# Two convolution layers on Trainium2: an order pinned around each pair of tiles, and first-image sums of squares on ScalarE

## The chip, the cores and the metric

The kernel runs on one core of one Trainium2 chip. The metric is the device time of one execution in microseconds (us). A core has these engines, each with its own instruction queue that is worked through in order: TensorE (PE in the profile; its weight loads are listed as PEld), VectorE (DVE), ScalarE (ACT), GpSimd (POOL), and SyncE (SP), which here only issues DMAs. Matmul results go to PSUM; everything else lives in SBUF. Engines wait for one another through semaphores.

## The reference

The network adds four "pre-activation" layers to x, which has shape (4, 8, 512, 512): four images of eight channels.

```
x = x + L0(gn(x))       # spiking attention block
x = x + L1(gn(x))       # 13x13 depthwise convolution
x = x + L2(gn(x))       # 3x3 convolution on values rounded to integers
x = x + L3(gn(x))       # 3x3 convolution in float32

def gn(v, G=4, eps=1e-5):          # group norm: per image, over 2 channels x 512 x 512
    m, s = mean(v), var(v)
    return (v - m) / sqrt(s + eps)

def L2(x):
    sx, sw = 127 / max|x|, 127 / max|weight|
    return conv3x3(clip(round(x * sx)), clip(round(weight * sw))) / (sx * sw) + bias
```

The change lies in layers 2 and 3, and touches nothing before them. Layer 3 of an image needs the mean and the variance of the whole image after layer 2, for each group of channels.

## The kernel before

**Tiles.** Layers 2 and 3 cut each image into 85 windows of 8 rows by 8 channels (64 partitions); two windows make a tile of 128 partitions by 512 columns, and two tiles (a and b) make a pair. An image has 22 pairs, the last of which has one half-filled tile. In this text pair 2.7 is pair 7 of image 2, counted from 0, and n = 22 t + p numbers the pairs over all images: 88 in all.

**One pair through layer 2.** `load` (L951) brings the pair in, six pairs deep. `normalise` makes two copies on GpSimd that undo a column permutation (u, L965; four buffers) and one normalisation over both tiles on ScalarE (y, L969; two buffers). `quantise` rounds y to integers in bf16 on VectorE (xq, L980; three buffers). `layer2` multiplies each tile with a banded weight matrix in 6 matmuls (L997) into PSUM (three banks), and VectorE then scales each result and adds it to u (L1003, `scalar_tensor_tensor`), which leaves the pair's result in x3, a ring of 26 pairs. Statistics of that result: for tile a, `bn_stats` on VectorE (L1014); for tile b, a row sum that L1003 writes out on the side, and a row sum of squares from an `activation` with `Square` on ScalarE (L1009).

**Layer 3.** When an image is through, `norm3` (L1047 to L1078, with the helper at L175 to L195) turns the statistics into a mean, a scale, and scaled weights (band_t). `layer3` of a pair sets two edge columns (L1089, GpSimd), runs 12 float32 matmuls (the profile shows each as two, so 24 lines of L1096), and ScalarE adds a constant (o, L1105; ten buffers); SyncE stores the result (L1112). Rows that neighbouring windows share are exchanged inside x3 by DMAs that GpSimd issues (L1143).

**The loop.** One Python loop over n (L1122) traces, in this order: the load of pair n+5, `normalise` of n+2, `quantise` of n+1, `layer2` of n, and, from n = 25 on, `layer3` of pair n-25. So layer 3 of image t runs beside layer 2 of image t+1, and layer 3 of image 3 is left for the end. The build does not keep the order of the trace: it places each engine's instructions by its own estimate, within data dependences and within edges that the source asks for. `tc.issue_after(op)` asks for such an edge: what is traced in its block stands behind `op` on the engine of `op`. It is an order in the queue alone, no wait. Before, `layer2` of n stands behind `normalise` of n+2 on ScalarE and behind `quantise` of n+1 on VectorE; nothing keeps these two from being placed earlier still.

**What reuse of buffers ties together.** L1003 of pair n writes the ring place that layer 3 of pair n-26 has read, so it waits for those matmuls. The first tile of pair n+2 takes the PSUM bank that L1003 left with tile b of pair n.

Of the kernel before, what the change touches and what calls it, by code (L numbers as in the profile page):

```python
# [42 lines left out]
P = 128  # L43
# [768 lines left out]
def weights23(tc, i, pool, scratch, ps_1, ident):  # L812


    nc = tc.nc

    def col(name, n=1):
        return pool.tile([P, n], F32, name=name)

    n_taps = 3 * B  # L820
    w = {}
    c24 = pool.tile([n_taps, i["c24"].shape[1]], F32, name="c24")
    nc.scalar.dma_start(c24, i["c24"])
    w2 = pool.tile([n_taps, n_taps], F32, name="w2t")
    nc.scalar.dma_start(w2, i["w2"])
    w3 = pool.tile([n_taps, n_taps], F32, name="w3t")
    nc.scalar.dma_start(w3, i["w3"])
    w["b2"], b3 = col("b2"), col("b3")
    nc.scalar.dma_start(w["b2"], i["b2"])
    nc.scalar.dma_start(b3, i["b3"])  # L830
    w["b23"] = col("b23")
    nc.vector.tensor_add(w["b23"], w["b2"], b3)

    def banded(taps, dtype, name, firsts):

# [15 lines left out]
        return band  # L851

    w["band3"] = band3 = banded(w3, F32, "band3", (-1, 1))
    w["sum3"] = pool.tile([P, 2, HALF], F32, name="sum3")
    nc.vector.tensor_add(w["sum3"], band3[:, :, 0, :], band3[:, :, 1, :])
    nc.vector.tensor_add(w["sum3"], w["sum3"], band3[:, :, 2, :])
    w["eye3"] = pool.tile([P, 2, 3, HALF], F32, name="eye3")
    nc.vector.memset(w["eye3"], 0.0)  # L860
    nc.vector.tensor_add(
        w["eye3"][:, 0, 1, B:], ident[:, : HALF - B], ident[:, HALF : P - B]
    )
    nc.vector.tensor_add(
        w["eye3"][:, 1, 1, : HALF - B], ident[:, B:HALF], ident[:, HALF + B :]
    )

    wall = scratch.tile([P, 2, D], F32, tag="y", name="wall")
    wall = wall.rearrange("p n d -> p (n d)")[:, : n_taps * n_taps]
    nc.scalar.dma_start(wall, bass.AP(i["w2"].tensor, 0, [[0, P], [1, n_taps * n_taps]]))  # L870
    w["sw"] = sw = col("sw")
    nc.vector.tensor_reduce(sw, wall, AX.X, ALU.max, apply_absolute_value=True)
    nc.vector.reciprocal(sw, sw)
    nc.vector.tensor_scalar_mul(sw, sw, MAX_Q)
    nc.vector.tensor_scalar_mul(w2, w2, sw[:n_taps])
    nc.vector.tensor_scalar(w2, w2, MAX_Q, -MAX_Q, op0=ALU.min, op1=ALU.max)
    nc.vector.tensor_scalar(w2, w2, ROUND, ROUND, op0=ALU.add, op1=ALU.subtract)
    w["band2"] = banded(w2, BF16, "band2", (0,))


    w["xq"] = [pool.tile([P, 2, D + 4], BF16, name=f"xq_{j}") for j in range(3)]
    for xq in w["xq"]:
        nc.gpsimd.memset(xq, 0.0)
    w["st3"] = [pool.tile([P, W2_N, 6], F32, name=f"st3_{j}") for j in range(2)]
    for st3 in w["st3"]:
        nc.gpsimd.memset(st3, 0.0)

    w["sums"] = [pool.tile([P, 2, N_PAIRS], F32, name=f"sums_{j}") for j in range(2)]
    w["inv"] = col("inv")
    w["m"], w["r"] = col("m_own", T), col("r_own", T)  # L890
    w["mr"] = col("mr_own", T)
    return w


def layers23(
# [80 lines left out]
    def quantise(t, p):  # L976
# [6 lines left out]
        ready[t, p] = u, xq  # L983
        return op.ins

    def layer2(t, p):
        ks = tiles(p)
        n_p = HALF * len(windows(ks[-1]))
        u, xq = ready.pop((t, p))
        s0 = slot(t, p)  # L990
        st3 = w["st3"][t % 2]
        for j, k in enumerate(ks):
            ps = ps_2.tile([P, D], F32, tag="conv2", name="ps_conv2")
            for dx in range(3):
                for a, _ in windows(k):
                    half = slice(a * HALF, (a + 1) * HALF)
                    mm = nc.tensor.matmul(  # L997
                        ps[half, :], lhsT=w["band2"][half, 0, dx, :], rhs=xq[half, j, dx + 1 : dx + 1 + D],
                        start=dx == 0, stop=dx == 2,
                    )  # L1000
            own = x3[:n_p, s0 + j, 1 : D + 1]
            sums = w["sums"][t % 2][:, :, p : p + 1]
            nc.vector.scalar_tensor_tensor(  # L1003
                own, ps[:n_p, :], w["inv"][:n_p], u[:n_p, j, :], op0=ALU.mult, op1=ALU.add,
                accum_out=sums[:, 0, :] if j else None,
            )
            if j:
                square = wpool.tile([P, D], BF16, tag="square", name="square")
                nc.scalar.activation(  # L1009
                    square, own, AF.Square, bias=w["m"][:, t : t + 1], scale=-1.0,  # L1010
                    accum_out=sums[:, 1, :],
                )
            else:
                nc.vector.bn_stats(st3[:n_p, k, :], own)  # L1014
        return mm.ins

    pairs = x3[:, :, 1 : D + 1].rearrange("p (n j) d -> p n j d", j=2)
# [24 lines left out]
    def norm3(t):  # L1042


        st3 = w["st3"][t % 2]
        total, squares = (w["sums"][t % 2][:, j, : N_PAIRS - 1] for j in range(2))
        nc.vector.tensor_scalar_mul(total, total, 1.0 / D)  # L1047
        for h in range(2):
            nc.vector.tensor_copy(st3[:, 1::2, 3 * h + 1], total)
        nc.vector.tensor_scalar(total, total, w["m"][:, t : t + 1], None, op0=ALU.subtract)  # L1050
        nc.vector.tensor_mul(total, total, total)
        nc.vector.scalar_tensor_tensor(
            total, total, -1.0 * D, squares, op0=ALU.mult, op1=ALU.add
        )
        for h in range(2):
            nc.vector.tensor_scalar_mul(st3[:, 1::2, 3 * h + 2], total, 0.5)
        st3 = st3.rearrange("p k (h z) -> p (k h) z", z=3)
        nc.vector.tensor_scalar_add(st3[:, :, 1], st3[:, :, 1], w["b2"])  # L1058
        m, r = yield from group_steps(
            st3.unsqueeze(1), 1, W2_N * 2, mask2, avg_same, ps_1, f"x3_{t}"  # L1060
        )
        zero = wpool.tile([P, 1], F32, tag="zero", name="zero")
        nc.vector.tensor_sub(zero, m, w["b2"])
        band = wpool.tile([P, 2, 3, HALF], F32, tag="band", name="band_t")
        nc.vector.scalar_tensor_tensor(
            band, w["band3"], r, w["eye3"], op0=ALU.mult, op1=ALU.add
        )
        scaled = wpool.tile([P, 1], F32, tag="scaled", name="scaled")
        nc.vector.tensor_mul(scaled, zero, r)
        yield  # L1070
        ps = ps_1.tile([P, 1], F32, tag="misc", name="ps_const")
        for a in range(2):
            half = slice(a * HALF, (a + 1) * HALF)
            nc.tensor.matmul(
                ps[half, :], lhsT=w["sum3"][half, a, :], rhs=scaled[half, :], start=True, stop=True
            )
        const = wpool.tile([P, 1], F32, tag="const", name="const")
        nc.vector.tensor_sub(const, w["b23"], ps)  # L1078
        norms[t] = zero, band, const
        yield  # L1080
# [37 lines left out]
    n_chunk = N_PAIRS // 2  # L1118
    copies, at_once = [], 0
    n_all = T * N_PAIRS  # L1120
    norms, norm = {}, iter(())
    for n in range(n_all + N_PAIRS + LAG):  # L1122
        if n < n_all:
            for m in range(6) if n == 0 else [n + 5]:
                if m < n_all:
                    load(*divmod(m, N_PAIRS))


            for m in range(3) if n == 0 else [n + 2]:
                if m < n_all:  # L1130
                    first = normalise(*divmod(m, N_PAIRS))
            for m in range(2) if n == 0 else [n + 1]:
                if m < n_all:
                    then = quantise(*divmod(m, N_PAIRS))
            with tc.issue_after(first), tc.issue_after(then):
                did = layer2(*divmod(n, N_PAIRS))
        next(norm, None)
# [49 lines left out]
```

## Time and profile before

| what | value |
| --- | --- |
| time, median of 3 runs (lowest to highest) | 3051.62 us (3049.63 to 3054.68) |
| the profiled execution's own time | 3049.44 us |
| its span, first to last instruction | 3047.7 us |
| layer 0: 0 to 2131 us of the span | PE busy 2093.4 of 2131.0 us |
| layer 1: 2131 to 2582 us | PE busy 449.0 of 451.0 us |
| layer 2 of image 0, and its statistics: 2582 to 2683 us | PE busy 50.1, DVE 92.0, ACT 51.8, POOL 70.7 of 101.0 us |
| layer 2 of images 1 to 3 beside layer 3 of images 0 to 2: 2683 to 2983 us | PE busy 261.8, DVE 208.4, ACT 192.2, POOL 195.2 of 300.0 us |
| layer 3 of image 3: 2983 to 3047.7 us | PE busy 59.7 of 64.7 us |

The span is the time between the first and the last instruction that the profiler recorded; the execution's own time is 1.7 us longer. "Busy" is the time in which an engine works on at least one instruction. The table says where to look: in layers 0 and 1 TensorE has next to no idle time, and the change leaves them alone. In the first image of layer 2 VectorE is the busy engine. In the 300 us that follow TensorE is busiest and yet idle for 38 us.

### The profile page before, as it was taken

What the parts mean: (1) busy time and instruction counts of PE and PEld (TensorE: products, weight loads), DVE (VectorE), ACT (ScalarE), POOL (GpSimd) and SP (SyncE); (2) the same over time, 40 slices, a digit from 0 to 9 for tenths busy, and PEclk for the clock granted to TensorE, in tenths of its full rate; (3) what the DMA queues carried; (4) which work ended last, traced back from release to release, by engine and by line L of the source; (5) the groups of instructions that cost most, each with busy time, mean ns of one, the idle gap of its engine ahead of it and who ended that gap; (6) DMA issues with size and microseconds to landing.
All of it is one profiled execution on the core that took longest, in us unless ns stands there. A gap on an engine that the chain in (4) does not pass through costs nothing. (4 is left out here: it accounts for less than half of the span.)

```text
span 3047.7 us, 38741 instructions
## 1 busy us (share of the span) xinstructions
PE 2913.9 (96%) x13993; PEld 1459.5 (48%) x13993; DVE 2228.9 (73%) x3793; ACT 542.5 (18%) x825; POOL 1042.9 (34%) x1963
## 2 busy tenths in 40 slices
PE   8999999999999999999999999998999999478989
PEld 6455555555555555555555555554433333134443
DVE  5997688688779868868876876886455556967860
ACT  1400010010000001000001000100111111556764
POOL 1242233333234323323322432333111112766751
PEclk9999999999999999999999999999999999999999
DMA  5221222212211222111121111112877778798985
GB/s 184 78 81 64 77 63 64 70 63 70 70 63 63 71 66 75 61 66 63 63 70 43 57 50 50 57 36 73 211 215 204 217 204 226 131 190 211 227 195 153
DMA packets 275703, 327.37 MB, mean 107 GB/s; under 512 B 23601, under 2 KB 171193, under 8 KB 275286
## 3 DMA queue, kind: packets, MB, share of 16 engines
q1 hardware_dynamic: 211930, 235.77, 28.4%
q0 software_dynamic: 23776, 62.35, 7.4%
q10 hardware_dynamic: 39803, 26.77, 2.9%
q8 instruction: 110, 1.80, 0.2%
q14 instruction: 84, 0.68, 0.1%
HBM read 210.60 MB, written 103.17 MB: 103 GB/s over the span
## 5 line engine op out<-in xcount | busy, mean ns | idle before, releaser
L464 PE MATMUL ps_in<-w_v,xn 128*128 128x512 f32 x1024 | 460.9, 599 | 2.4 <-issue 2.2
L464 PE MATMUL ps_in<-w_k,xn 128*128 128x512 f32 x1024 | 450.2, 593 | 1.0 <-DVE v_k L429 0.7
L464 PE MATMUL ps_in<-xn,w_q 128*128 128x512 f32 x1024 | 449.6, 592 | 0.1
L750 PE MATMUL ps_conv<-x,bt 112*64 112x512 f32 x2048 | 444.6, 593 | 0.0
L500 PE MATMUL ps_b<-toep,vtok 128*64 128x512 bf16 x3072 | 370.1, 381 | 0.1
L412 ACT ACTIVATE h_q<-v_q,c_half 128x512 f32<-128x512 f32 x96 | 69.3, 722 | 1543.2 <-DVE v_q L408 1378.9
L549 POOL COPY x1s<-x1s 128x2 f32<-128x2 f32 (+1 forms) x1024 | 227.0, 277 | 295.9 <-DVE x1s L538 295.9
L437 POOL TENSOR_TENSOR h_v<-h_v,c_v 128x512 f32<-128x512 f32 x96 | 123.2, 1283 | 574.4 <-DVE h_v L436 539.9
L527 PE MATMUL ps_out<-wp,so 128*128 128x512 f32 x1024 | 308.9, 444 | 0.0
L464 PEld LDWEIGHTS ps_in<-w_k,xn 128*128 128x128 f32 x1024 | 194.1, 190 | 222.4 <-issue 205.0
L464 PEld LDWEIGHTS ps_in<-xn,w_q 128*128 128x128 f32 x1024 | 191.8, 190 | 220.1 <-issue 212.7
L464 PEld LDWEIGHTS ps_in<-w_v,xn 128*128 128x128 f32 x1024 | 189.8, 190 | 216.3 <-issue 210.6
L750 PEld LDWEIGHTS ps_conv<-x,bt 112*64 112x64 f32 x2048 | 149.7, 135 | 286.3 <-issue 285.8
L500 PEld LDWEIGHTS <-vtok 128*64 128x64 bf16 x3072 | 208.6, 110 | 123.4 <-issue 2.3
L1096 PE MATMUL ps_conv<-x,band_t 64*64 64x512 f32 x2040 | 264.0, 605 | 1.4 <-ACT o L1105 1.4
L527 PEld LDWEIGHTS ps_out<-wp,so 128*128 128x128 f32 x1024 | 192.6, 188 | 94.1 <-issue 58.3
L965 POOL COPY u<-x 128x512 f32<-128x512 f32 (+1 forms) x172 | 196.6, 1175 | 106.6 <-issue 48.2
L997 PE MATMUL ps_conv<-xq,band 64*64 64x512 bf16 x1020 | 140.4, 396 | 67.4 <-DVE xq L980 41.6
L538 DVE SCALAR_TENSOR_TENSOR x1s<-v_p,xr 128x256 f32<-128x256 f32 x256 | 186.5, 768 | 15.1 <-DMA x<-x1s 3.8
L766 POOL DMA_DIRECT2D x<-xo x128 | 71.5, 565 | 339.9 <-ACT xo L757 325.5
L195 POOL TENSOR_TENSOR grstd_x<-grstd_x,neg_half 128x1 f32<-128x1 f32 (+1 forms) x28 | 21.6, 771 | 463.2 <-DVE grstd_x L194 457.3
L757 ACT ACTIVATE xo<-ps_conv,off 128x512 f32<-128x512 f32 x128 | 88.0, 687 | 445.8 <-PE ps_conv L750 411.8
(182 smaller groups left out, 3636.7 us busy)
## 6 DMA issues: line engine op xcount, KB each, us to landing
x<-x SPq DMA_DIRECT2D x64, 917.0 KB
x<-x SPq DMA_DIRECT2D x168, 256.0 KB
x<-x1s POOLq DMA_DIRECT2D x128, 262.0 KB, 2.5
x<-in_x SPq DMA_DIRECT2D x128, 256.0 KB
xr<-in_x SPq DMA_DIRECT2D x128, 256.0 KB
out<-o SPq DMA_DIRECT2D x164, 192.0 KB
xs<-in_x SPq DMA_DIRECT2D x112, 256.0 KB
x<-xo ACTq DMA_DIRECT2D x128, 128.0 KB
```

Source lines behind the costliest of these rows:

```text
L437: nc.gpsimd.tensor_add(h, h, c_twice[n])
L464: mm = nc.tensor.matmul(ps, lhsT=lhsT, rhs=rhs, start=k == 0, stop=k == NC - 1)
L500: nc.tensor.matmul(pb[two * DH : (two + 1) * DH, :], lhsT=v[:, c, h * DH : (h + 1) * DH], rhs=toep[z][:, h, u : u + N], start=c == 0 and z ...
L527: nc.tensor.matmul(ps, lhsT=so[:, k, c * P : (c + 1) * P], rhs=wpT[z][:, k, :], start=k == 0 and z == 0, stop=k == NC - 1 and z == 1,)
L538: nc.vector.scalar_tensor_tensor(own, v.rearrange("p (g v) -> p g v", g=PH)[:, two, :], 1.0, by_phase[:, two, :], op0=ALU.is_ge, op1=ALU.add,)
L549: nc.gpsimd.tensor_copy(x1[:, f, u : u + n], x1[:, fm, um - n + 1 : um + 1][:, ::-1])
L750: nc.tensor.matmul(ps[q * M1 : (q + 1) * M1, :], lhsT=bt[:, z, :], rhs=xt[:, w0 : w0 + N_PS1, z : z + NV], start=z == 0, stop=z == SHIFTS - 1,
L757: nc.scalar.activation(xo[:, a, :], ps, AF.Identity, bias=off[:, t : t + 1])
L766: engine.dma_start(bass.AP(dst.tensor, dst.offset + (q * n_half * W1_OUT * B + b) * D + f * NV, [[B * D, W1_OUT], [W1_OUT * B * D, n_half] ...
L965: nc.gpsimd.tensor_copy(u[:n_p, j, :].rearrange("p (v g) -> p v g", g=PH), x[:, j, :].rearrange("p (g v) -> p v g", g=PH),)
L997: mm = nc.tensor.matmul(ps[half, :], lhsT=w["band2"][half, 0, dx, :], rhs=xq[half, j, dx + 1 : dx + 1 + D], start=dx == 0, stop=dx == 2,)
L1096: nc.tensor.matmul(ps[j][b * HALF : (b + 1) * HALF, :], lhsT=band[half, b, dx, :], rhs=x3[half, s0 + j, dx : dx + D], start=dx == 0, stop= ...
```

## The change

Two things change.

First, `done` keeps the last VectorE instruction and the last ScalarE instruction of each pair's `layer2`. `normalise` and `quantise` of the next turn of the loop are now traced behind both. Together with the edges that were there, `quantise` of n+1 stands between the results of pair n-1 and those of pair n on VectorE, and `normalise` of n+2 between the squares of pair n-1 and of pair n on ScalarE.

Second, in image 0 every tile but the last takes its statistics from the two sums, L1003's and ScalarE's, and not every second tile. 21 `bn_stats` leave VectorE, 21 squares come to ScalarE. In images 1 to 3 tile a keeps `bn_stats`. The arrays for the sums grow from 22 to 43 columns, and `norm3` works on 42 columns in image 0, on 21 in the others.

```diff
@@ weights23
-    w["sums"] = [pool.tile([P, 2, N_PAIRS], F32, name=f"sums_{j}") for j in range(2)]
+    w["sums"] = [pool.tile([P, 2, W2_N], F32, name=f"sums_{j}") for j in range(2)]
@@ layers23
+    def by_sums(t):
+        return range(0 if t == 0 else 1, W2_N - 1, 1 if t == 0 else 2)
+
@@ layer2
-            sums = w["sums"][t % 2][:, :, p : p + 1]
-            nc.vector.scalar_tensor_tensor(
+            sums = w["sums"][t % 2][:, :, k : k + 1]
+            summed = k in by_sums(t)
+            done["DVE"] = nc.vector.scalar_tensor_tensor(
                 own, ps[:n_p, :], w["inv"][:n_p], u[:n_p, j, :], op0=ALU.mult, op1=ALU.add,
-                accum_out=sums[:, 0, :] if j else None,
-            )
-            if j:
+                accum_out=sums[:, 0, :] if summed else None,
+            ).ins
+            if summed:
                 square = wpool.tile([P, D], BF16, tag="square", name="square")
-                nc.scalar.activation(
+                done["ACT"] = nc.scalar.activation(
                     square, own, AF.Square, bias=w["m"][:, t : t + 1], scale=-1.0,
                     accum_out=sums[:, 1, :],
-                )
+                ).ins
             else:
-                nc.vector.bn_stats(st3[:n_p, k, :], own)
+                done["DVE"] = nc.vector.bn_stats(st3[:n_p, k, :], own).ins
@@ norm3 (and the same slice in the four copies into st3)
-        total, squares = (w["sums"][t % 2][:, j, : N_PAIRS - 1] for j in range(2))
+        ks = by_sums(t)
+        ks = slice(ks.start, ks.stop, ks.step)
+        total, squares = (w["sums"][t % 2][:, j, ks] for j in range(2))
@@ the loop
-            for m in range(3) if n == 0 else [n + 2]:
-                if m < n_all:
-                    first = normalise(*divmod(m, N_PAIRS))
-            for m in range(2) if n == 0 else [n + 1]:
-                if m < n_all:
-                    then = quantise(*divmod(m, N_PAIRS))
+            with ExitStack() as order:
+                for op in done.values():
+                    order.enter_context(tc.issue_after(op))
+                for m in range(3) if n == 0 else [n + 2]:
+                    if m < n_all:
+                        first = normalise(*divmod(m, N_PAIRS))
+                for m in range(2) if n == 0 else [n + 1]:
+                    if m < n_all:
+                        then = quantise(*divmod(m, N_PAIRS))
```

What the build makes of it on VectorE shows best as a list of its queue. q is the rounding (L980), s the scale-and-add (L1003) of tile a or b, b the `bn_stats` (L1014):

```
image 0, before: q0.5 s0.4a s0.4b b0.4   q0.6 s0.5a s0.5b b0.5   q0.7 ...
image 0, after:  q0.5 s0.4a s0.4b        q0.6 s0.5a s0.5b        q0.7 ...
image 1, before: q1.8 s1.6a b1.6 s1.6b   q1.9 s1.7a b1.7 s1.7b   q1.10 ...
image 1, after:  q1.7 s1.6a b1.6 s1.6b   q1.8 s1.7a b1.7 s1.7b   q1.9 ...
```

TensorE's queue is the same in both but for one place in image 2 and one in image 3, where five matmuls of layer 2 move behind one pair of layer 3. ScalarE's queue is the same in most of images 1 to 3; in image 0 two squares now stand between two normalisations, and the normalisation stands one pair later. On GpSimd one exchange DMA and one pair of copies swap places; on SyncE one load and one store do.

More of the change, by code (lines that the diff above doesn't have):

```diff
@@ L1045, in norm3 @@
         st3 = w["st3"][t % 2]
-        total, squares = (w["sums"][t % 2][:, j, : N_PAIRS - 1] for j in range(2))
+        ks = by_sums(t)
+        ks = slice(ks.start, ks.stop, ks.step)
+        total, squares = (w["sums"][t % 2][:, j, ks] for j in range(2))
         nc.vector.tensor_scalar_mul(total, total, 1.0 / D)
         for h in range(2):
-            nc.vector.tensor_copy(st3[:, 1::2, 3 * h + 1], total)
+            nc.vector.tensor_copy(st3[:, ks, 3 * h + 1], total)
         nc.vector.tensor_scalar(total, total, w["m"][:, t : t + 1], None, op0=ALU.subtract)
@@ L1055, in norm3 @@
         for h in range(2):
-            nc.vector.tensor_scalar_mul(st3[:, 1::2, 3 * h + 2], total, 0.5)
+            nc.vector.tensor_scalar_mul(st3[:, ks, 3 * h + 2], total, 0.5)
         st3 = st3.rearrange("p k (h z) -> p (k h) z", z=3)
@@ L1120, in layers23 @@
     n_all = T * N_PAIRS
-    norms, norm = {}, iter(())
+    norms, norm, done = {}, iter(()), {}
     for n in range(n_all + N_PAIRS + LAG):
```

## The prediction

> **What bounds the kernel now.** I read the window sums first. Layers 0 and 1 keep TensorE busy and are untouched, so everything is decided after 2582 us. There I took four stretches (columns: window, its length, busy time of PE, PEld, DVE, ACT, POOL with counts, granted PE clock, DMA share, GB/s):
>
> ```profile
> 2593.00:2661.00 68.00, 34.57 (x255) 13.78 (x255) 65.83 (x106) 41.48 (x63) 53.62 (x47) 0.95 0.71 134
> 2702.40:2725.30 22.90, 17.03 (x146) 8.26 (x147) 11.36 (x20) 12.85 (x20) 11.78 (x15) 1.00 0.84 193
> 2731.50:2770.40 38.90, 38.90 (x355) 21.29 (x349) 35.04 (x57) 31.71 (x52) 31.87 (x42) 1.00 0.82 208
> 2899.10:2922.00 22.90, 17.08 (x148) 8.23 (x144) 13.10 (x23) 12.86 (x20) 11.77 (x15) 1.00 0.97 196
> ```
>
> The first is image 0 of layer 2: VectorE is full. The third is a loose stretch (pairs 1.12 to 1.21): TensorE is full, a pair takes 3.9 us. The second and fourth are tight stretches (pairs 1.6 to 1.10 and 3.7 to 3.10): no engine is full. The chain of waits says why (start, duration, what):
>
> ```profile
> 2902.70 0.76 DVE x L1003
> ...
> 2903.49 0.69 DVE st L1014
> 2904.18 0.67 DVE x L1003 x2
> ...
> 2904.90 0.62 PE ps_conv L997 x4
> ...
> 2905.73 2.65 PE ps_conv L1096 x22
> 2908.38 0.03 issue
> 2908.41 0.76 DVE x L1003
> ```
>
> It is a circle between two engines, 5.71 us a turn: result a of pair n, bn_stats, result b, the first tile of pair n+2 in layer 2, layer 3 of pair n-25, then result a of n+1, which waits for that layer 3 because it overwrites a ring place. TensorE idles twice a turn, 0.91 us for result a and 0.55 us for result b. The timeline shows where the rounding stands:
>
> ```profile
> 2901.20 0.74 DVE L980 TENSOR_SCALAR xq<-y 128x1024 bf16<-128x1024 f32 x1 [1.47 <-ACT y L969]
> 2902.70 0.75 DVE L1003 SCALAR_TENSOR_TENSOR x<-ps_conv,inv,u 128x512 f32<-128x512 f32 x1 [0.76 <-PE ps_conv L1096]
> 2904.90 0.62 PE L997 MATMUL ps_conv<-xq,band 64*64 64x512 bf16 x4 [0.55 <-DVE x L1003]
> ```
>
> The L980 at 2901.20 is q3.9, ahead of result 3.7a: it runs while VectorE waits for layer 3, free of charge. Image 0 in the same view:
>
> ```profile
> 2613.37 0.68 DVE L1014 BATCH_NORM_STATS2 st<-x 128x6 f32<-128x512 f32 x1
> 2613.57 2.56 POOL L965 COPY u<-x 128x512 f32<-128x512 f32 x2 [0.51 <-issue]
> 2613.98 1.22 DVE L980 TENSOR_SCALAR xq<-y 128x1024 bf16<-128x1024 f32 x1
> 2615.11 1.40 DVE L1003 SCALAR_TENSOR_TENSOR x<-ps_conv,inv,u 128x512 f32<-128x512 f32 x2
> 2616.16 1.24 ACT L969 ACTIVATE y<-u,mr_own,r_own 128x1024 f32<-128x1024 f32 x1 [1.12 <-POOL u L965]
> ```
>
> VectorE has no gap: 0.61 (bn_stats, start to start) + 1.13 + 1.33 = 3.07 us a pair. The rounding takes 1.22 us here and 0.74 above: it waits for a GpSimd copy.
>
> [...] rounding 0.74 against 1.22 us, two copies 2.56 against 2.1 us. [...]
>
> ```profile
> 2693.62 0.84 PE L997 MATMUL ps_conv<-xq,band 64*64 64x512 bf16 x6 [1.26 <-DVE x L1003]
> 2696.00:2698.00 2.00, 2.00 (x16) 0.96 (x12) 0.71 (x1) 0.99 (x1) 2.00 (x4) 0.50 1.10 172
> 2773.45 0.38 PE L178 MATMUL gps_x<-gsum_x,avg_same 128*128 128x1 f32 x2 [2.95 <-DVE gsum_x L175]
> 2773.76 4.47 PE L1096 MATMUL ps_conv<-x,band_t 64*64 64x512 f32 x24
> ```
>
> Idle gaps of 1.26 and 0.55 us, close together, were followed by half clock at 2696; the turns with 0.91 and 0.55 were not. [...] a tiny matmul of norm3 (L178) waited 2.95 us with layer 3 behind it, and that layer 3 then took 4.47 us, not 2.8.
>
> **The change, part by part**, against the profiled execution (3049.44 us; span 3047.7).
>
> *Image 0, 21 bn_stats away, 21 squares added.* VectorE then needs at most 1.13 + 1.33 + two accumulator reads of 0.08, some 2.6 us a pair. ScalarE needs two squares of 0.72 (start to start) and a normalisation of 1.23: 2.67. [...] So ScalarE is next, at 2.67, 0.40 below 3.07. Pairs 0.2 to 0.10 are nine: 3.6 us. The first pair's bn_stats and the last full pair's give 0.6 each. At 2629.34 a rounding stood 2.76 us behind GpSimd's first exchange DMA and two copies, and that pair took 4.6 us; rounding would come first there: 1.5. For the nine pairs after that GpSimd also issues an exchange DMA each (0.62): 2.6 + 0.6 is no less than the 3.1 they take now, except that GpSimd is up to four pairs ahead and can give that lead away: between 0 and 3.6, I take 0.2. Total -6.5; ends -3 and -9.5. The normalisation, now behind two squares, has a slack of a pair (y of n+2 is wanted at n+2's rounding, a pair later). norm3 on 42 columns instead of 21: six instructions of 0.2 us, under 0.5, taken as 0.
>
> *The rounding pinned, tight stretches.* The built order puts q of n+2 behind result b of n, where before it stood ahead of result a; TensorE's order is as it was, so the first tile of n+2 stays ahead of layer 3 of n-25 and now waits for that rounding too. Result b starts 1.40 into the turn and the next instruction 0.66 later; the rounding takes 0.70 [...], and 0.05 to TensorE: 2.81 instead of 2.20. So +0.61 a turn, +0.69 if the accumulator read stands in between. Turns: six in image 1 (pairs 1.5 to 1.10; in 1.4 the second rounding already stood on the path), four each in images 2 and 3, and one more each (2.6, 3.6) where bn_stats too now precedes the rounding, +1.25. 14 x 0.65 + 2 x 1.25 = 11.6; taken 11.5, ends +9 and +19 (a copy first in every turn, 0.5 each). Behind the waiting matmul stands layer 3, and for it wait ScalarE's output and the next result: nothing hides it.
>
> *The clock.* The idle pair becomes 0.91 and 1.16 us, 2.07 in all, above the 1.81 that was followed by half clock and above the 1.46 that was not. A half-clock window cost 1.7 us (pair 1.6 took 7.41, not 5.71). [...] 16 turns, 3 times, +5; ends 0 and +12.
>
> *Between images.* One rounding fewer stands ahead of result 2.2 and its like, which waited for GpSimd's copies behind norm3, and result 1.20 no longer waits for a 2.02 us rounding of 2.0. That can take up to 2.4 of the 2.95 us at 2770.5 and the slow matmuls behind it (1.7), and 1.15 at 2870.6. On the other side, normalisation of 2.1 now waits for a square. Taken -3, ends -6 and +1. A gap of 1.43 us at 2956.6 goes as well, but TensorE waits 3.87 us soon after for statistics that wait for output DMAs: 0.
>
> *Loose stretches:* TensorE is full, the rounding has over 3 us to spare: 0. The one swap on GpSimd's and on SyncE's queue: 0, either neighbour is at hand.
>
> Sum: -6.5 + 11.5 + 5 - 3 = +7.0. On the profiled execution that is 3056.4; this lies 2.2 us under the median, so the median forecast is 3051.6 + 7.0 = 3058.6.
>
> **Rivals.** (1) The clock holds in the tight stretches. The place is pairs 1.5 to 1.10 and their like; price 0 instead of 5; it decides if no window of the new turn falls to half speed: +2, 3053.6, not slower. For it: image 0 kept full clock with TensorE busy 45% of the time. Against it: the drop at 2695. (2) Image 0 runs at 2.67 us throughout and both gaps between images go with their slow matmuls, while the turn grows by the least: -9.5 - 6 + 9 = -6.5, 3045, faster. For it: GpSimd's lead. Against it: eight exchange DMAs, and DMA shares over 1 from 2650. (3) [...] the clock falls six times: -6.5 + 15.5 + 10 - 3 = +16, 3068. For it: a copy that waits for a load (3.33 us before the copies at 2905.61) starts anywhere. (4) That the pins do nothing is excluded by the built order.
>
> **Numbers.** A measurement of this kernel tells 0.2%, 6.1 us, from no change. The forecast (+4 to +13) gets 0.55, of which 0.42 lies above 6.1 and 0.13 below; rival 1 gets 0.20 (no change), rival 2 0.12 (faster), rival 3 0.13 (slower). Slower 0.55, same 0.33, faster 0.12. The range, 3046 to 3069, reaches from near rival 2 to rival 3 and leaves out about a tenth on each side; the forecast's own is 3055 to 3065.
>
> **What would show it.** In the changed profile: pairs of image 0 at about 2.7 us, then 3.1 with the exchange DMAs; layer 3 starting near 2676 instead of 2683; turns of 6.3 to 6.4 us in the tight stretches with TensorE waiting for L980 in place of L1003 before the first tile; some half-clock windows there; loose stretches at 3.9. I am wrong if the turn stays at 5.7 or image 0 stays at 3.1.

## The result, and the profile after

The changed kernel takes 3052.92 us (median; 3051.45 to 3056.78), the kernel before 3051.38 us in the same comparison: ratio 1.0006, 95% interval 0.9988 to 1.0023. That is no change that can be measured. The forecast was 3058.6 with "slower" as the likeliest case, so the time lies inside the range, but the likeliest case did not come. The two profiled executions differ by 2.0 us in span (3049.7 against 3047.7).

Behind these 2 us stand gains and losses of over 14 us each. I cut both traces at the starts of the same results (3.11a is tile a of pair 3.11; all in us):

| stretch | before | after | difference | forecast |
| --- | --- | --- | --- | --- |
| start of layer 2 (first normalisation) | 2592.48 | 2593.66 | +1.2 | 0 |
| image 0: first normalisation to result 0.20a | 67.03 | 58.70 | -8.3 | -6.5, with the next |
| 0.20a to 1.4a | 27.26 | 28.41 | +1.2 | |
| 1.4a to 1.11a, tight | 42.61 | 47.60 | +5.0 | +16.5 for the three |
| 1.11a to 2.6a | 71.27 | 68.54 | -2.7 | -3 with 2.11a to 3.6a |
| 2.6a to 2.11a, tight | 28.43 | 33.31 | +4.9 | |
| 2.11a to 3.6a | 68.65 | 70.03 | +1.4 | |
| 3.6a to 3.11a, tight | 28.43 | 33.34 | +4.9 | |
| 3.11a to 3.21a | 41.18 | 37.40 | -3.8 | 0 with the next |
| 3.21a to the end of the span | 80.36 | 78.71 | -1.7 | |

The start of layer 2 belongs to layers 0 and 1, which the change doesn't touch, so its 1.2 us are scatter between two executions.

The window sums of the changed kernel (columns as in the prediction: PE, PEld, DVE, ACT, POOL, then clock, DMA share, GB/s), for image 0 (two windows), a tight stretch and a loose one:

```profile
2601.60:2624.10 22.50, 13.99 (x114) 5.60 (x110) 21.61 (x47) 22.50 (x46) 22.50 (x19) 1.00 0.72 191
2595.00:2625.00 30.00, 20.05 (x144) 8.16 (x144) 27.23 (x57) 28.69 (x55) 25.63 (x21) 0.91 0.57 153
2906.00:2919.00 13.00, 9.40 (x81) 3.95 (x76) 5.42 (x10) 6.42 (x10) 6.35 (x8) 1.00 0.95 214
...
2936.50:2959.50 23.00, 23.00 (x218) 10.80 (x214) 18.58 (x31) 20.13 (x35) 19.77 (x25) 1.00 0.79 173
```

In image 0 ScalarE is now the fullest engine (28.69 of 30 us), and from 2601.6 to 2624.1 us, where the pairs are evenly paced, neither it nor GpSimd has a gap (22.50 of 22.50 us each). In the tight stretch no engine is full. In the loose one TensorE is full, 3.88 us a pair.

The chain of waits through a tight turn of the changed kernel:

```profile
2906.55 0.76 DVE x L1009
...
2907.34 0.69 DVE st L1020
2908.03 0.66 DVE x L1009 x2
2908.69 0.62 DVE xq L982
...
2909.35 0.62 PE ps_conv L1002 x4
...
2910.19 2.66 PE ps_conv L1104 x22
...
2912.88 0.76 DVE x L1009
```

It is the circle of before with one more link: the rounding (L982) stands between result b and the next first tile, and TensorE waits for it, as the timeline has it:

```profile
2909.35 0.62 PE L1002 MATMUL ps_conv<-xq,band 64*64 64x512 bf16 x4 [1.16 <-DVE xq L982]
```

From one result a to the next it is 6.33 us; it was 5.71.

Two windows of 2 us of the same kernel show TensorE's clock in one of these turns:

```profile
2694.00:2696.00 2.00, 0.84 (x6) 0.27 (x5) 1.97 (x5) 0.96 (x3) 0.32 (x1) 1.00 0.93 264
2696.00:2698.00 2.00, 1.78 (x12) 1.02 (x16) 0.17 (x1) 1.60 (x3) 2.00 (x2) 0.56 0.83 147
```

After a window with 0.84 us of matmuls in 2 the clock falls to half (0.56 over the second window, 0.50 from 2696.25 to 2699.60 us), and that turn takes 8.0 us. It happens in four of the 17 tight turns, for 3.4 us each time (a half-clock window below), here named by the pair at their end (1.7, 1.10, 2.9, 3.11); before it was one.

Image 0 of the changed kernel, where GpSimd begins to issue exchange DMAs (timeline):

```profile
2624.61 0.75 POOL L1154 DMA_DIRECT2D x<-x  x1
...
2625.37 4.11 POOL L967 COPY u<-x 128x512 f32<-128x512 f32 x4
...
2626.69 3.35 DVE L982 TENSOR_SCALAR xq<-y 128x1024 bf16<-128x1024 f32 x1
```

Behind the issue GpSimd runs four copies in a row, and a rounding that takes 0.7 us where no copy is in its way (0.69 at 2631.30) takes 3.35. Copies in a row alone didn't do that: from 2608.4 to 2616.0 us GpSimd runs six of them without a pause, and the roundings among them take 1.1 us. Pair 0.12 then takes 4.81 us; long roundings also come at 0.15 (4.81) and 0.18 (4.43). The other full pairs of image 0 take 2.0 to 2.6 us. The long roundings leave TensorE gaps of 3.31, 3.21 and 2.07 us, and its clock falls to half (0.50) in image 0 too, from 2631.4, 2638.2 and 2648.4 us on: the layer 2 matmuls between 2624 and 2652 us take 516 ns in the median. What that costs there was not measured. In the kernel before a gap of 3.12 us at 2629.0 was not followed by half clock (1.00 from 2599.7 to 2661.0 us).

### The profile page after: what moved, and what is told of

Read it like the earlier page. It is cut to its first block, busy times and chain, and to the rows that moved or that the text cites. A ratio compares the mean times of both kernels' runs of the same rounds, so it can differ in the third digit from the quotient of the medians.

```text
span 3049.7 us, 38814 instructions
## 1 busy us (share of the span) xinstructions
PE 2917.8 (96%) x13993; PEld 1459.2 (48%) x13993; DVE 2223.0 (73%) x3793; ACT 554.2 (18%) x867; POOL 1042.9 (34%) x1963
## 5 line engine op out<-in xcount | busy, mean ns | idle before, releaser
L967 POOL COPY u<-x 128x512 f32<-128x512 f32 (+1 forms) x172 | 203.9, 1219 | 109.3 <-issue 66.2
L1009 DVE SCALAR_TENSOR_TENSOR x<-ps_conv,inv,u 128x512 f32<-128x512 f32 (+1 forms) x172 | 123.1, 743 | 84.6 <-PE ps_conv L1104 64.4
```

The lines of the kernel that those rows point to most:

```text
L967: nc.gpsimd.tensor_copy(u[:n_p, j, :].rearrange("p (v g) -> p v g", g=PH), x[:, j, :].rearrange("p (g v) -> p v g", g=PH),)
L1009: done["DVE"] = nc.vector.scalar_tensor_tensor(own, ps[:n_p, :], w["inv"][:n_p], u[:n_p, j, :], op0=ALU.mult, op1=ALU.add, accum_out=sums[ ...
```

## Experiments

All are edits of the changed kernel and compute the whole reference, but for the two that say otherwise.

### The two halves of the change, and the two pins, apart

Without pins, which is to say without the new edges behind `done` (sums only):

```diff
-                for op in done.values():
+                for op in ():
```

> The changed kernel without the pins: image 0's squares stay on ScalarE, the rounding and the normalisation go where the built order puts them, in the tight stretches ahead of result a. Computes the whole reference. My theory (the pinned rounding lengthens the tight turn, the squares shorten image 0): pairs 0.2 to 0.11 at 2.5 to 2.6 us as in the changed kernel, tight turns back at 5.7 us, at most two half-clock windows; the tight stretches give back 14.8 us, but the 5.4 us after image 3's tight stretch and part of the 2.7 us between images 1 and 2 come back, so about 3045 us (6 to 8 below the kernel before). Rival A (the pins pace image 0): pairs of image 0 return to 3.07 us, about 3052. Rival B (the squares on ScalarE lengthen the turn, by delaying what the result waits for): turns stay at 6.3 us, about 3053 or more.

Measured: 3042.68 us (3038.15 to 3044.01), ratio to before 0.9971, interval 0.996 to 0.9981: faster. Image 0 takes 58.81 us to result 0.20a, tight turns are back at 5.71 us, with no half-clock window. Rivals A and B fall.

Pins only:

```diff
-        return range(0 if t == 0 else 1, W2_N - 1, 1 if t == 0 else 2)
+        return range(1, W2_N - 1, 2)
```

> The changed kernel with image 0's statistics as before (bn_stats on one tile of two, squares on the other), pins on both sides kept. Computes the whole reference. My theory: image 0 at 3.07 us a pair, so about 6.5 us of the changed kernel are lost there; tight turns 6.35 us with about four half-clock windows; about 3058 to 3060 us, 0.2% above the kernel before. Rival A (the pins pace image 0): pairs at 2.5 us, about 3053. Rival B (the squares lengthen the turn): turns at 5.7 us, about 3038 to 3045.

Measured: 3061.21 us (3057.77 to 3061.76), ratio 1.0032, interval 1.0021 to 1.0044. Image 0 is back at 67.06 us, tight turns take 6.33 us, five of them with half clock. Against the runs of before, the sums alone bring -0.29% (about -9 us) and the pins alone +0.32% (about +10): together the +1 to +2 us that the whole change shows.

Only the pin on VectorE (rounding behind result b):

```diff
-                for op in done.values():
+                for op in [done[e] for e in done if e == "DVE"]:
```

> The changed kernel with the pin on VectorE's result alone (the rounding stands behind result b, the normalisation goes where the built order puts it). Computes the whole reference. My theory (the rounding is what lengthens the turn): turns 6.35 us with about four half-clock windows, image 0 at 2.55 us, about 3053 us as the changed kernel. Rival (the normalisation behind the square lengthens the turn, because the rounding waits for it): turns at 5.7 us, about 3040.

Measured: 3052.09 us (3050.86 to 3055.61), ratio 1.0006, interval 0.9998 to 1.0014. Stretch by stretch it is the changed kernel: none of the table's from image 0 to 3.21a differs by more than 0.12 us. So once the rounding is pinned, the pin on the normalisation does nothing; the rival falls.

Only the pin on ScalarE (normalisation behind the square):

```diff
-                for op in done.values():
+                for op in [done[e] for e in done if e == "ACT"]:
```

> The changed kernel with the pin on ScalarE's square alone (the normalisation stands behind the square of pair n; the rounding goes where the built order puts it, which in the tight stretches is ahead of result a as in the kernel before, and in the loose stretches one behind each pair without the two roundings in a row at 1.20, 2.20 and 3.20). Computes the whole reference. My theory: turns 5.7 us, image 0 at 2.55 us, the gains between images (2.7 us) and after image 3's tight stretch (5.4 us) mostly kept, because they come from the order of roundings there: about 3037 to 3041 us, the fastest of the four. Rival (the normalisation's pin lengthens the turn): turns 6.3 us, about 3053. Second rival (the gain after image 3 comes from the rounding's pin): turns 5.7 us but about 3045.

Measured: 3051.78 us (3050.53 to 3053.95), ratio 1.0006, interval 0.9998 to 1.0014. I was half right. The tight turns are 5.71 us, but the total is 11 to 15 us over what I expected, and most of that stands in the loose stretches, which now take 4.14 us a pair instead of 3.88. The timeline of this kernel in a loose stretch:

```profile
2739.98 0.72 ACT L1015 ACTIVATE square<-x,m_own 128x512 bf16<-128x512 f32 x1 [1.05 <-issue]
...
2740.70 1.23 ACT L971 ACTIVATE y<-u,mr_own,r_own 128x1024 f32<-128x1024 f32 x1
...
2741.96 0.75 DVE L982 TENSOR_SCALAR xq<-y 128x1024 bf16<-128x1024 f32 x1 [1.46 <-ACT y L971]
...
2742.63 1.40 DVE L1009 SCALAR_TENSOR_TENSOR x<-ps_conv,inv,u 128x512 f32<-128x512 f32 x2
...
2744.13 0.72 ACT L1015 ACTIVATE square<-x,m_own 128x512 bf16<-128x512 f32 x1 [1.06 <-DVE x L1009]
```

Square, normalisation, rounding, results, square: the normalisation of n+2 is held behind the square of n-1, while the rounding of n+2, no longer held, stands ahead of result a of n and waits for it (1.46 us). This pin without the other closes a new circle, of VectorE and ScalarE, 4.14 us long. With both pins the rounding comes a pair later and finds y ready.

### Where in the turn the pin costs, and what gives image 3's end its even pace

Pins off in the tight stretches alone:

```diff
-                for op in done.values():
+                for op in () if n > N_PAIRS and n % N_PAIRS in range(4, 12) else done.values():
```

> The changed kernel with the pins taken off for the loop turns n whose pair number p is 4 to 11 in images 1 to 3, so the rounding in the tight stretches stands ahead of result a again, and everywhere else it stays pinned. Computes the whole reference. My theory (the pin costs only where a turn is a circle of VectorE and TensorE, and in the loose stretches it brings the regular 3.88 us that the changed kernel shows after pair 3.12): tight turns 5.71 us, no more than one half-clock window, image 0 at 2.55 us, and the loose stretch of image 3 (pairs 3.12 to 3.21) about 37.4 us as in the changed kernel instead of 39.9 to 41.2 without pins; about 3035 to 3038 us. Rival (the regular loose stretch comes from the state in which the pinned tight stretch leaves the queues): loose stretch of image 3 back at 40 us, about 3041 to 3043, as the kernel without pins.

Measured: 3041.11 us (3038.6 to 3045.07), ratio 0.9974, interval 0.9963 to 0.9985. The tight turns are 5.71 us, without half clock, as expected. But the rival has the rest: 3.11a to 3.21a takes 40.25 us, not 37.4, although the roundings there are pinned as in the changed kernel. The even end of image 3 is therefore no work of the pins in it.

The statistics of tile a moved behind the pinned rounding:

```diff
-                done["DVE"] = nc.vector.bn_stats(st3[:n_p, k, :], own).ins
+                late.append((st3[:n_p, k, :], own))
...
+            with tc.issue_after(then):
+                for st, own in late:
+                    nc.vector.bn_stats(st, own)
+            late.clear()
             with tc.issue_after(first), tc.issue_after(then):
                 did = layer2(*divmod(n, N_PAIRS))
```

(After the last pair of an image they are issued at once.)

> The changed kernel with bn_stats of tile a moved from between results a and b to behind the next pinned rounding. Computes the whole reference. My theory (TensorE waits for result a, statistics, result b and rounding in a row, so 0.68 us off that row is 0.6 to 0.7 us off every tight turn, and the pair of idle gaps of TensorE falls below what half clock follows): tight turns 5.65 to 5.75 us, none or one half-clock window in them instead of four, about 3053 - 16 x 0.65 - 4 x 1.65 = 3036 us. Rival A (the rounding waits for something else[...]): turns stay above 6.2 us, about 3053. Rival B (half clock has to do with the length of the pinned turn and not with the idle gaps): turns shorter but half-clock windows stay, about 3042.

Measured: 3035.76 us (3034.07 to 3041.76), ratio 0.9958, interval 0.9943 to 0.9973. The chain of waits of this kernel:

```profile
2800.12 1.42 DVE x L1009 x3
2801.54 0.62 DVE xq L982
...
2802.20 0.62 PE ps_conv L1002 x4
...
2803.03 2.69 PE ps_conv L1104 x22
...
2805.75 1.41 DVE x L1009 x2
```

and its window over the tight stretch of image 1, with the clock in the third last column:

```profile
2685.00:2717.00 32.00, 24.73 (x218) 10.60 (x217) 14.60 (x29) 18.06 (x29) 18.92 (x25) 1.00 0.95 212
```

The turn is 5.61 to 5.64 us in images 1 and 2, 0.7 less than 6.33; in image 3 four turns take 5.86 to 5.94. The rounding is as long as before and as firmly pinned, and there is no half-clock window left in the tight stretches: TensorE's idle gaps are 0.93 and 0.43 us a turn here (0.93 and 0.74 at most, in image 3). So each link of the circle counted in full here (statistics of 0.69 us moved, 0.7 us off the turn), and half clock followed the idle gaps, not the pin. Rivals A and B fall. That the total met the forecast of 3036 us is partly luck: the tight stretches gave 17.6 us, the stretch behind them in image 3 took 8.6 back (46.02 instead of 37.40), and the stretches between images gave 5.1 more.

### The circle itself

TensorE's queue, as built, has the first tile of pair n+2 ahead of layer 3 of pair n-25 in the tight stretches only. To take that lead away, `layer3` keeps its last matmul in `done["PE"]`, and `layer2` is issued behind it:

```diff
-            with tc.issue_after(first), tc.issue_after(then):
+            with ExitStack() as order:
+                for op in [first, then] + [done[e] for e in done if e == "PE"]:
+                    order.enter_context(tc.issue_after(op))
                 did = layer2(*divmod(n, N_PAIRS))
```

> The changed kernel, pins kept, with one more order: layer 2's matmuls of pair n are issued behind layer 3's last matmul of the loop turn before (pair n-26), so that TensorE's queue no longer has the first tile of pair n+2 ahead of layer 3 of pair n-25. Computes the whole reference. My theory (the tight stretches exist because of that lead of TensorE's queue; without it the circle is broken and the pinned rounding costs nothing, as in the loose stretches): pairs 1.5 to 1.11, 2.6 to 2.11 and 3.6 to 3.11 at 3.9 to 4.2 us instead of 6.3 and 8.0, no half-clock windows there; the three stretches shrink from 47.6 + 34.1 + 34.1 us to about 28 + 20 + 20; about 3005 to 3010 us. Rival A (DMA becomes the bound: tight stretches already show shares of 0.84 to 0.97 of the DMA engines at 5.7 us a pair): pairs about 4.8 to 5.5 us there, about 3020 to 3030. Rival B (the ring place alone sets it, whatever TensorE's order): turns stay at 6.3 us, about 3053.

> The same order of TensorE without the pins: squares of image 0 on ScalarE, rounding and normalisation where the built order puts them. Computes the whole reference. My theory (without a circle the place of the rounding matters little, but the two roundings in a row behind 1.20, 2.20 and 3.20 come back): 2 to 6 us more than with the pins, about 3008 to 3014 us; image 0 at 2.55 us. Rival (the rounding ahead of result a helps here too): faster than with the pins by 5 us or more.

Measured: with the pins 3030.15 us (3029.0 to 3035.64), ratio 0.9943, interval 0.9926 to 0.996; without them 3031.44 us (3027.89 to 3034.05), ratio 0.994, interval 0.9926 to 0.9955. Both beat the kernel before and the changed one, and the pins make no difference between them that these runs can tell (I had expected 2 to 6 us). The chain of waits of the first, in what was a tight stretch:

```profile
2888.31 2.58 PE ps_conv L1104 x22
2890.89 1.08 PE ps_conv L1002 x10
2891.97 0.15 PE ps_conv L1104
2892.12 0.07 PE ps_conv L1002
2892.19 2.57 PE ps_conv L1104 x22
```

The chain is TensorE alone: no link on VectorE, 3.88 us a pair. The three tight stretches take 25.4, 26.6 and 19.4 us instead of 47.6, 33.3 and 33.3: 43 us saved. Yet the span falls by 22.6. The rest is lost in later stretches: 3.11a to 3.21a takes 50.07 us instead of 37.40 and 2.11a to 3.6a 78.56 instead of 70.03; inside the tight stretch of image 2, pair 2.10 alone takes 10.42. Not all of the 50.07 is stalls: 22 more matmuls of layer 3 and 8 more of layer 2 fall into it, 3.2 us by estimate (36 matmuls take 3.88 us), and 6.8 us of it run at half clock. The groups of waits of this kernel between 2660 and 2960 us (total, times, longest):

```profile
ACT o L1114 <- DMA out<-o: 50.0, 35, 3.9
POOL u L967 <- DMA x<-x: 37.4, 16, 6.0
```

In the changed kernel neither of the two waits occurs in this time. The engines have become fast enough to wait for the transfers. That was rival A, though it is not an even slower pace as I had it but stalls of 4 to 6 us.

### Are the transfers the next bound?

Layer 3's output DMAs carry half of the columns, so half of the output is not written, once on the kernel with TensorE's order and once on the changed kernel:

```diff
-                out[t, :, row : row + n, :].rearrange("c r w -> r c w"), o[at : at + n * B, :]
+                out[t, :, row : row + n, : D // 2].rearrange("c r w -> r c w"), o[at : at + n * B, : D // 2]
```

> The changed kernel with TensorE's order (layer 2 of pair n behind layer 3 of pair n-26), and with layer 3's output DMAs carrying only the left half of the columns, so half of the output is not written; every other instruction and wait is as in that kernel. My theory (with TensorE's circle gone, the transfers are the bound: ScalarE waited 50.0 us for output DMAs and GpSimd 37.4 us for loads between 2660 and 2960 us, with 0.92 of the DMA engines' time taken): both waits fall below 15 us, the long stalls at pairs 2.10, 3.16 and 3.19 (8 to 10 us each) go, and the time is about 3008 to 3015 us instead of 3030. Rival (the stalls come from the order of the queues, above all SyncE's, where loads stand behind outputs that wait for ScalarE): the stalls stay, the time is 3024 us or more.

> The changed kernel as it is, with layer 3's output DMAs carrying only the left half of the columns, so half of the output is not written. My theory (the pinned tight stretches are a circle of VectorE and TensorE and take no time from transfers; there ScalarE waited for no output DMA at all after 2660 us): tight turns stay at 6.33 us with about four half-clock windows, the loose stretch of image 3 stays at 37.4 us, and only the last output DMAs at the end and the statistics that wait behind outputs between images get shorter: about 3043 to 3051 us, 2 to 10 below the changed kernel. Rival (transfers set the pace in the changed kernel too): about 3030 us or less.

Measured: with TensorE's order 3012.24 us (3011.59 to 3014.91), ratio 0.988, interval 0.9863 to 0.9896: 18 us less than with whole outputs. The changed kernel: 3054.71 us (3050.64 to 3057.1), ratio 1.0013, interval 1.0007 to 1.002, so nothing gained; I had expected 2 to 10 us. The same transfers are worth 18 us in one kernel and nothing in the other. My expectation on the waits was a miss: they fell to 32.9 and 25.8 us, not below 15, and pairs 3.16 and 3.19 still take 7.0 and 6.5 us. The 10.42 us at 2.10 are gone. Of the 17.3 us that the span lost, 14.3 lie between 2.6a and 3.6a; 3.11a to 3.21a still takes 47.59 us. So bytes alone don't make the stalls of image 3, and the rival, the order of SyncE's queue, stands there: by the trace SyncE spends 263 of the 300 us between 2660 and 2960 us on its DMA instructions, with whole outputs and with halved ones. No run tests it.

### Exchange DMAs on SyncE's queue

In image 0's loop turns alone:

```diff
-            nc.gpsimd.dma_start(*copies.pop(0))
+            (nc.sync if n < N_PAIRS else nc.gpsimd).dma_start(*copies.pop(0))
```

> The changed kernel with the exchange DMAs of image 0's loop turns issued by SyncE instead of GpSimd. Computes the whole reference. My theory (in image 0 a rounding that comes up while GpSimd issues an exchange DMA stands behind that issue and the two copies after it, which gave the roundings of 3.35, 3.29 and 2.75 us and the pairs of 4.81, 4.81 and 4.00 us): those three pairs take 2.5 to 2.7 us, no rounding over 1.3 us, image 0 ends 5 to 6 us earlier; layer 3 is taken that much earlier too, about 3047 us. Rival (the long roundings come with the traffic of the exchange itself, or with the copies alone): the long pairs stay, about 3053 us.

Measured: 3042.98 us (3035.25 to 3045.86), ratio 0.9976, interval 0.9969 to 0.9982. Pairs 0.12 to 0.18 take 2.53 to 2.55 us, and image 0 is 4.7 us shorter (54.00 us to result 0.20a). The same place in its timeline, where the layer 2 matmuls are back at 376 ns:

```profile
2626.63 7.67 POOL L967 COPY u<-x 128x512 f32<-128x512 f32 x6
2627.27 1.00 DVE L982 TENSOR_SCALAR xq<-y 128x1024 bf16<-128x1024 f32 x1 [0.19 <-ACT y L971]
```

GpSimd's copies run without a pause here, and the roundings pass between them in 1.0 us. So in image 0 neither copies alone nor the exchange itself held a rounding for three microseconds: with the DMA issue on GpSimd it took up to 3.35 us, with the issue on SyncE no rounding between 2624 and 2652 us took more than 1.49. The rival falls. The rest of this kernel's time can't be put down to this: TensorE's queue came out in another order, with no tight stretch in image 1, and pair 1.4 takes 13.5 us, with GpSimd waiting 7.2 us for a load.

All exchange DMAs, on the kernel with TensorE's order:

```diff
-            nc.gpsimd.dma_start(*copies.pop(0))
+            nc.sync.dma_start(*copies.pop(0))
```

> The changed kernel with TensorE's order (layer 2 of pair n behind layer 3 of pair n-26), and with all exchange DMAs issued by SyncE instead of GpSimd. Computes the whole reference. My theory (transfers are the bound once the circle is gone, and GpSimd's queue takes 2.6% of the DMA engines' time per MB against 1.3% for SyncE's between 2660 and 2960 us): image 0 as with the last kernel, the stalls for loads and outputs (37.4 and 50.0 us of waits) at least halve, about 3012 to 3020 us instead of 3030. Rival (SyncE's queue keeps its order, so loads and outputs stand behind exchange DMAs that wait for results, or the cost belongs to the transfer and not to the queue): 3028 us or more.

Measured: 3108.89 us (3105.61 to 3113.65), ratio 1.02, interval 1.0184 to 1.0215. A clear miss. The DMA queues between 2660 and 2960 us (packets, MB, share of the time of 16 engines), in the kernel with GpSimd's queue:

```profile
q1 hardware_dynamic: 29790, 54.20, 68.6%
q0 software_dynamic: 5817, 8.87, 23.3%
```

and with all on SyncE's:

```profile
q1 hardware_dynamic: 30426, 55.26, 73.3%
```

On GpSimd's queue 23.3% for 8.87 MB is 2.6% of the engines' time per MB, and loads and outputs on SyncE's took 1.3%. All transfers together took 1.46% per MB, and with the exchanges on SyncE's queue 1.33%: the cost by byte fell, but in a slower kernel, and the exchanges' own share can't be read from the mixture. The time came out on the rival's side: GpSimd now waits 103.1 us for loads, against 37.4. Its reason, that loads stand behind exchanges that are not ready, is not shown: between 2660 and 2960 us SyncE's queue waited 4.9 us ahead of exchanges and 80.7 us ahead of outputs, and with the exchanges on GpSimd's queue already 74.7 us ahead of outputs. Why the loads come so much later stays open.

## Why the prediction was right or wrong

**Image 0, -6.5: right in sum, by two errors that cancel.** By result 1.4a image 0 had brought -7.2 (-8.3 and +1.2), and layer 3 starts at 2677.6 us, where 2676 was forecast. ScalarE is full, as forecast, but at 2.54 us a pair, not 2.67: two squares of 0.70 and a normalisation of 1.13, start to start, instead of 0.72 and 1.23. GpSimd has no gap there either, and no run separates the two. Against that, the step "rounding would come first there: 1.5" failed: the long rounding did not go, it came three times (3.35, 3.29, 2.75 us), and these three pairs took 6.4 us more than three at the pace of 2.54, of which the pairs behind them won back a part. The run with SyncE's queue, 4.7 us shorter there, shows the cause there to be the DMA issue on GpSimd. In the traces of before and of the changed kernel 33 of the 34 roundings of over 1.4 us end 0.55 to 0.61 us behind the end of a GpSimd copy. Through two copies with no issue between them, and none for 2.4 us ahead, a rounding took 2.47 us (2787.15); the six of over 2.7 us all have a DMA issue on GpSimd beside them or up to 1.4 us ahead. Two of image 0's three waited through the rest of three copies behind an issue, the third (2.75 us) through a copy, an issue and another copy. Why that is so stays open.

**Pinned rounding, +11.5 (9 to 19): right, at its low end.** The turn is 6.33 us, forecast 6.3 to 6.4, and TensorE waits for L982 ahead of the first tile. Less the half-clock windows the three stretches lost 9.9 us. The missing 1.6 are a miscount. In images 2 and 3, behind the one turn that lost 1.3 us, three lost 0.6 each and not four (the turn into 2.11 and 3.11 took 6.30 us before already), and the turn into 1.5 lost 0.3 instead of 0.65. The kernels with one pin show that it is the rounding, and the kernel with moved statistics that every link counted (0.7 us off the turn for 0.69 us moved).

**Clock, +5: right, with an estimated rate.** Three more half-clock windows at 1.65 us, +4.9. Over four kernels with the pinned turn (the changed one, both with the rounding's pin, and the one with half outputs) 18 of 68 tight turns had one; over four with turns of 5.6 to 5.9 us, none. The forecast's three in 16 turns was the author's estimate; measured is one in four. Gaps of 0.93 and 1.16 us with matmuls between went ahead of it, and went without it in the other turns: what decides between them was not shown.

**Between images, -3: -1.4.** Inside the range given (-6 to +1), but not for the reason given. The gap at the first statistics went down from 2.95 to 2.57 us only, and the second rose from 1.15 to 2.42. All idle gaps of TensorE in the two stretches together rose, from 3.65 to 3.76 us and from 2.73 to 3.61. What moved the times is in part a half-clock window of 3.4 us, which left the first stretch and came in the second; about 1.1 us less in each is left unexplained.

**"A gap of 1.43 us at 2956.6 goes as well, but TensorE waits 3.87 us soon after for statistics that wait for output DMAs: 0", and "loose stretches: 0": this is the step that failed.** From 3.11a to the end the changed kernel gained 5.4 us, and this is most of why +7.0 became +2. I took the end as fixed by transfers and by TensorE, and did not ask what a later arrival does to them. TensorE's gaps there in the kernel before, and the first matmuls of layer 3 behind them:

```profile
2952.82 3.30 PE L1096 MATMUL ps_conv<-x,band_t 64*64 64x512 f32 x22 [0.89 <-ACT o L1105]
2957.98 0.62 PE L997 MATMUL ps_conv<-xq,band 64*64 64x512 bf16 x4 [1.43 <-DVE x L1003]
2969.76 0.58 PE L178 MATMUL gps_x<-gsum_x,avg_same 128*128 128x1 f32 x2 [3.87 <-DVE gsum_x L175]
2972.56 10.90 PE L1096 MATMUL ps_conv<-x,band_t 64*64 64x512 f32 x72
```

and in the changed kernel:

```profile
2973.41 0.38 PE L178 MATMUL gps_x<-gsum_x,avg_same 128*128 128x1 f32 x2 [2.52 <-DVE gsum_x L175]
2975.80 9.65 PE L1104 MATMUL ps_conv<-x,band_t 64*64 64x512 f32 x72
```

The gap of 1.43 us went, as forecast, but so did the one of 0.89, and the 3.87 that was to swallow the gain fell to 2.52 itself: 3.7 us. The rest is the clock: before, half clock was granted from 2968.3 to 2978.5 us, in the changed kernel for 3.4 us alone, so the same 72 matmuls take 1.25 us less and the tiny ones of norm3 0.4 less. Together this is 5.3 of the 5.4 us; less idle time and the loss by half clock, TensorE needs 110.1 us from 3.11a to the end in both.

What stood behind the gaps shows in the chain of waits of the kernel before:

```profile
2939.03 7.95 DMA out<-o
...
2949.72 3.21 DMA out<-o
...
2957.18 0.81 DVE x L1003 x2
...
2958.18 7.91 DMA out<-o
2966.13 0.81 ACT square L1009 x2
...
2967.44 0.65 DVE x L1003
```

ScalarE waits for an output to land, and with it the normalisations and squares in its queue, and so the results and statistics. In the changed kernel the chain from 2933 to 2971 us is TensorE alone. ScalarE's waits for outputs between 2900 and 2985 us (total) beside the stretch 3.11a to 3.21a, ordered by when result 3.11a starts (all in us):

| kernel | 3.11a starts | ScalarE waits for outputs | TensorE idle in the stretch | 3.11a to 3.21a |
| --- | --- | --- | --- | --- |
| TensorE's order | 2903.3 | 17.7 | 5.3 | 50.07 |
| TensorE's order, no pins | 2907.9 | 19.9 | 7.9 | 44.94 |
| statistics last | 2908.3 | 16.7 | 4.8 | 46.02 |
| pins off in tight stretches | 2917.9 | 9.2 | 2.2 | 40.25 |
| image 0's exchanges on SyncE's queue | 2921.3 | 10.5 | 2.2 | 41.37 |
| sums only | 2923.7 | 6.2 | 2.7 | 39.93 |
| before | 2926.2 | 5.6 | 2.3 | 41.18 |
| pin on ScalarE only | 2931.1 | 0 | 0.6 | 39.17 |
| pin on VectorE only | 2932.9 | 6.1 | 0 | 37.50 |
| changed | 2933.6 | 0 | 0 | 37.40 |
| pins only | 2943.9 | 0 | 0 | 37.41 |

On the whole, the earlier the engines arrived in these kernels, the longer they waited for transfers (17.7 us at 2903.3, none at 2933.6). ScalarE's waits alone are no price: with the pin on VectorE only they are 6.1 us, and TensorE loses nothing. (With the pin on ScalarE only the new circle of 4.14 us sets the pace; two rows, TensorE's order with pins and statistics last, hold 6.8 us of half clock.) So part of what the pin took in the tight stretches was time that the kernel before gave away later, waiting for outputs. That the order of roundings is not the cause is shown by the kernel with pins off in the tight stretches. That transfers cost time in the fast kernels and none in the changed one is shown by halved outputs. That a later arrival is what ends the waits is read from this table; no run moves the arrival alone, and halved outputs were not tried on the kernel before. Why outputs land late for an early arrival stays open too: with TensorE's order and halved outputs, 3.11a at 2890.0, ScalarE still waits 15.4 us for them.

**The rivals.** Rival 1 lands nearest (3053.6), but its reason, a clock that holds, did not come. Rival 2 had the pace of image 0 and not the rest. Rival 3's six half-clock windows were four, and the 4 us in its 15.5 for GpSimd's copies ahead of the rounding did not come: the turn stayed at 6.33.

## What to carry to other kernels

Where two engines form a circle, what is put between two of its links can cost its full length (here 0.62 us of rounding made the turn 6.33 instead of 5.71 us), free as it is elsewhere (a loose pair took 3.9 us before and 3.88 with it); look first for the edge in a queue that closes the circle, since removing it (0.9943 of before) was worth at least as much as the best order of the links (0.9958). What is won or lost in one stretch is not the change in the total: ask what the next stretch waits for, above all transfers, and price an earlier or later arrival there. An order pinned on one of two instructions that depend on each other can close a new circle: here the pin on the first of them alone, the normalisation, did (4.14 us a pair), and the pin on the second alone, the rounding, did not. Look at both queues after such a pin.

## What was not expected of the hardware

A rounding on VectorE took 3.35 us behind GpSimd's copies after a DMA issue on GpSimd, and 1.0 us between copies that ran without a pause when SyncE issued that DMA. The exchange DMAs took 2.6% of the DMA engines' time per MB from GpSimd's queue, where loads and outputs on SyncE's took 1.3%; with all of them on SyncE's queue it was 1.3% for the mixture. In the tight turns half clock followed gaps of 0.93 and 1.16 us in about one turn of four (18 of 68), and in none of the turns with 0.93 and 0.74 or less.
